# Part of an expert layer's start, moved into the last attention batch of a fused cross-attention and feed-forward kernel

## The chip, the cores and the metric

The kernel runs on one core of one Trainium2 chip. The metric is the device time of one execution in microseconds. The engines have one instruction queue each: TensorE (PE in the profile; PEld is its weight load), VectorE (DVE), ScalarE (ACT), GpSimd (POOL) and SyncE (SP, which issues most transfers). An engine takes its instructions in the order of its queue and waits on semaphores for the other engines.

## The reference, cut to what matters

The whole model is two layers on x (8 batches of 256 rows of 512 values). The change lies in the second layer: cross-attention with 16 heads, and then a feed-forward layer with two shared experts that run on every row and sixteen routed ones, of which each row takes its best two.

```python
def _attend(q, k, v):
    scores = einsum('bqnd,bknd->bnqk', q, k) * scale
    return einsum('bnqk,bknd->bqnd', softmax(scores), v)
x = x + (_attend(q, k_img, v_img)) @ Wo + bo      # q, k: RMS norm of projections

h = layernorm(x)
aff = sigmoid(h @ wa)                             # affinities, 16 experts
topk_p, topk_i = top_k(aff, 2)                    # shares are normalised
expert(h) = (gelu(h @ g + gb) * (h @ w1 + b1)) @ w2 + b2
x = x + h + sum(shared experts of h) + sum(shares * routed experts of h)
```

In the code `h @ g` and `h @ w1` are called the gate and up products, `gp` and `up`; the affinities' product is `lg` (logits).

## The kernel before, in words

The program has four stages one after the other: a long convolution, a quantised feed-forward layer, attention, experts. Only the last two are touched.

**Attention** (from 414 us to 820 us) is 64 steps, eight for each of eight batches; a step is four heads of one 128-row tile against 256 keys. Steps are counted here from 0, so the last batch is steps 56 to 63. All four compute engines are held to program order (`in_order`), so the order in which the Python loop calls the parts is the order of each queue. One turn n of the loop calls, in this order:

- `normalise` of step n-1: a reciprocal on DVE (`rden`), then POOL multiplies the 128x1024 probabilities `pr` by it;
- `scores` of step n: 4 products on PE into `sc`, then on DVE a maximum over them and its scaling (both are `mx`);
- `turn` of step n-2: 8 transposes of `pr` on PE into two PSUM tiles `pt`, copied to `pts` by DVE and ACT, one each;
- `exps` of step n: four exponentials on ACT from `sc` to `pr`, which need `mx`;
- in the first six turns of a batch, a sixth of the projections for the batch after it (`coming.middle`, `coming.end`): `k_mm`, `q_mm`, `v_mm` and transposes. The last batch has none to make;
- `Norm` and its factor: layer-norm statistics of the batch that was finished before (in turns 6 and 7 of a batch);
- `values` of step n-3, in every even turn: products `o` on PE, copied to `oT` by ACT;
- `project_out`, in every fourth turn: product `fo` on PE, added to `xs` by DVE, bias added by POOL.

[...]

Behind the loop come the last batch's `Norm` and the end of all attention pools.

**Experts.** 16 tiles of 128 rows make four blocks (`tb`) of 512. The work up to the routed experts is, in PE order: `tiles_in(0)` and `tiles_in(1)` (each row tile is normalised by DVE to `dxn`, transposed by PE to `dxT`, copied by ACT into `xT`), `logits(0)` (product `lgT`, DVE copy `lgs`, product `lg`), the first gate and up products `gate_up(0, 0, 0)`, `tiles_in(2)`, `logits(1)`, `tiles_in(3)`, `logits(2)`, `logits(3)`; then seven more gate and up products of blocks 0 and 1, and `down`. Between them the generator `route` is drawn piece by piece: affinities (`aff`), the two maxima (`hot`), ranks by PE (`rank`), slots, and 32 scatters by POOL. `gated` applies gelu on ACT and the product on DVE (`yT`). The eight units of shared work are named by block, expert and half, so (0, 0, 1) is the second half of expert 0 on block 0.

Pools: attention works in a pool `att` with two buffers of everything; the first batch uses `first` and `second`, left from the stage before. The experts' pools `moe`, `experts` and PSUM `psD` are opened when attention's are closed.

Of the kernel before, what the change touches and what calls it, by code (L numbers as in the profile page):

```python
# [8 lines left out]
F32 = mybir.dt.float32  # L9
# [62 lines left out]
def tile_kernel(ctx: ExitStack, tc: tile.TileContext, a: dict, out: bass.AP):  # L72
# [743 lines left out]
    def biased(pool, nm, i, tok, bias, pre, ss):  # L816

        nc.vector.tensor_tensor(pre[:, i, :], tok, bias, ALU.add)
        junk = pool.tile([P, D], F32, tag="junk", name=f"{nm}_junk{i}")
        nc.scalar.activation(  # L820
            junk, pre[:, i, :], AF.Square, bias=zero, accum_out=ss[:, i : i + 1]
        )
# [26 lines left out]
    class Batch:  # L849
# [23 lines left out]
        def middle(self, k):  # L873
            b = self.b
            T = [xs[:, i, b, :] for i in range(2)]
            if k == 1:
                r = self.root.newton()
                self.xn = []
                for i in range(2):
                    self.xn.append(self.qpool.tile([P, D], F32, tag="xn", name=f"cxn{b}{i}"))  # L880
                    nc.vector.tensor_scalar(
                        self.xn[i], T[i], self.mv[:, i, 0:1], r[:, i : i + 1],
                        ALU.subtract, ALU.mult,
                    )
# [194 lines left out]
    with tc.tile_pool(name="att", bufs=2) as ap_, tc.tile_pool(  # L1079
        name="psC", bufs=2, space=PSUM  # L1080
    ) as pc:

        attention = in_order(tc)
        attention.__enter__()
# [4 lines left out]
        class Step:  # L1089
            def __init__(self, batch, i, cp, p, oT):  # L1090
                self.batch, self.b, self.i, self.cp, self.p, self.oT = batch, batch.b, i, cp, p, oT
                self.nm = f"{batch.b}{i}{cp}{p}"

            def scores(self):

                kT, qT = self.batch.kT, self.batch.qT
                self.sc = pc.tile([P, 2, 2, S], F32, tag="sc", name=f"sc{self.nm}")
                for cc in range(2):
                    for rr in range(2):
                        rows = slice((2 * self.p + rr) * NHD, (2 * self.p + rr + 1) * NHD)  # L1100
                        c = 2 * self.cp + cc
                        nc.tensor.matmul(  # L1102
                            self.sc[:, rr, cc, :], lhsT=qT[rows, c, self.i * P : (self.i + 1) * P],
                            rhs=kT[rows, c, :], start=True, stop=True,
                        )
                self.mx = stat.tile([P, 4], F32, tag="mx", name=f"mx{self.nm}")
                nc.vector.tensor_reduce(  # L1107
                    self.mx, self.sc.rearrange("p r c k -> p (r c) k"), AX.X, ALU.max
                )
                times(self.mx, self.mx, -scale)  # L1110

            def exps(self):
                self.pr = ap_.tile([P, 2, 2, S], F32, tag="pr", bufs=4, name=f"pr{self.nm}")
                self.den = stat.tile([P, 4], F32, tag="den", name=f"den{self.nm}")
                for h in range(4):
                    nc.scalar.activation(  # L1116
                        self.pr[:, h // 2, h % 2, :], self.sc[:, h // 2, h % 2, :], AF.Exp,
                        bias=self.mx[:, h : h + 1], scale=scale, accum_out=self.den[:, h : h + 1],
                    )

            def normalise(self):
                rden = stat.tile([P, 4], F32, tag="rden", name=f"rden{self.nm}")
                nc.vector.reciprocal(rden, self.den)  # L1123
                flat = self.pr.rearrange("p r c k -> p (r c) k")
                nc.gpsimd.tensor_tensor(  # L1125
                    flat, flat, rden.unsqueeze(2).to_broadcast([P, 4, S]), ALU.mult
                )

            def turn(self):

                self.pts = []
                for rr in range(2):
                    pt = pc.tile([P, 2, 2, P], F32, tag="tr", name=f"pt{self.nm}{rr}")
                    for cc in range(2):
                        for k in range(2):
                            nc.tensor.transpose(  # L1136
                                pt[:, cc, k, :], self.pr[:, rr, cc, k * P : (k + 1) * P], ident
                            )
                    pts = ap_.tile([P, 2, 2, P], F32, tag="pts", bufs=8, name=f"pts{self.nm}{rr}")
                    if rr:  # L1140
                        nc.scalar.copy(pts, pt)  # L1141
                    else:
                        nc.vector.tensor_copy(pts, pt)
                    self.pts.append(pts)

            def values(self, before):

                pts = before.pts + self.pts
                cp, v = self.cp, self.batch.v
                op = pc.tile([P, 2, P], F32, tag="mm", name=f"o{self.nm}")  # L1150
                for cc in range(2):
                    for k in range(2):
                        for r in range(4):
                            d0 = (4 * (2 * cp + cc) + r) * NHD
                            nc.tensor.matmul(
                                op[r * NHD : (r + 1) * NHD, cc, :], lhsT=v[:, k, d0 : d0 + NHD],
                                rhs=pts[r][:, cc, k, :], start=(k == 0), stop=(k == 1),
                            )
                nc.scalar.copy(self.oT[:, 2 * cp : 2 * cp + 2, :], op)

        def project_out(b, i, oT):
            T = xs[:, i, b, :]
            fo = pc.tile([P, D], F32, tag="mm", name=f"fo{b}{i}")
            for c in range(DC):
                nc.tensor.matmul(  # L1165
                    fo, lhsT=oT[:, c, :], rhs=wsb["Wo"][:, c, :], start=(c == 0), stop=(c == DC - 1)
                )
            nc.vector.tensor_tensor(T, T, fo, ALU.add)
            nc.gpsimd.tensor_tensor(T, T, wsb["bo"], ALU.add)

        class Norm:


            def __init__(self, b):
                self.at = slice(2 * b, 2 * b + 2)
                for i in range(2):
                    st = stat.tile([P, 6], F32, tag="bn", name=f"d{b}_bn{i}")
                    nc.vector.bn_stats(st, xs[:, i, b, :])
                    nc.vector.bn_aggr(dmv[:, 2 * b + i, :], st)
                self.root = Root(dmv[:, self.at, 1], 1.0, ln_eps, f"d{b}")  # L1180

            def factor(self):
                nc.vector.tensor_copy(dr[:, self.at], self.root.newton())
# [4 lines left out]
        batches[1].kpool = batches[1].qpool = ap_  # L1188
        batches[1].psum = pc
        steps = []  # L1190
        for b in range(B):
            for i in range(2):
                oT = ap_.tile([P, DC, P], F32, tag="oT", name=f"oT_{b}{i}")
                steps += [(b, i, cp, p, oT) for cp in range(2) for p in range(2)]
        for n in range(len(steps) + 4):
            coming = None
            k = n % 8
            if n < len(steps):
                if k == 0 and 0 < steps[n][0] < B - 1:
                    batches.append(Batch(steps[n][0] + 1, (ap_, ap_), pc))  # L1200
                steps[n] = Step(batches[steps[n][0]], *steps[n][1:])
                if k < 6 and steps[n].b + 1 < B:
                    coming = batches[steps[n].b + 1]
            if 0 < n <= len(steps):
                steps[n - 1].normalise()
            if coming:
                coming.begin(k)
            if k == 7 and n > 8:
                finished.root.log()
            if n < len(steps):  # L1210
                steps[n].scores()
            if 2 <= n < len(steps) + 2:
                steps[n - 2].turn()
            if n < len(steps):
                steps[n].exps()
            if coming:
                coming.middle(k)
                coming.end(k)
            if k == 6 and n > 8:
                finished = Norm((n - 14) // 8)  # L1220
            elif k == 7 and n > 8:
                finished.factor()
            if 3 <= n < len(steps) + 3 and steps[n - 3].p:
                steps[n - 3].values(steps[n - 4])
            if n >= 4 and steps[n - 4].cp and steps[n - 4].p:
                project_out(steps[n - 4].b, steps[n - 4].i, steps[n - 4].oT)
        finished = Norm(B - 1)
        finished.root.log()
        finished.factor()
# [326 lines left out]
    for (tb, e, f), n in zip(rest, (2, 2, 3, 3, 3, 3, 2)):  # L1556
        gated(tb, e, f, gate_up(tb, e, f, shw[e]), yTs[tb])
        for _ in range(n):
            next(pieces)
# [148 lines left out]
```

## Time and profile before

Median of three runs: 1248.28 us (1248.28 to 1249.29). The execution that was profiled took 1249.04 us; its span in the trace, from the first to the last instruction, is 1247.3 us, so 1.7 us lie around the span.

Over the span PE is busy 95%, DVE 60%, ACT 43%, POOL 35%. In stretches around the change, busy microseconds of each engine and the granted PE clock as a share of full speed:

| stretch, us | what runs | PE | DVE | ACT | POOL | PE clock |
|---|---|---|---|---|---|---|
| 480 to 540 (60 us) | attention, middle batches | 59.60 | 40.76 | 33.34 | 19.51 | 1.00 |
| 758 to 810 (52 us) | attention, mostly the last batch | 46.06 | 39.06 | 28.79 | 23.85 | 0.90 |
| 810 to 822 (12 us) | end of attention | 8.59 | 4.34 | 0.96 | 2.61 | 0.81 |
| 822 to 835 (13 us) | first tiles, first logits, (0, 0, 0) | 12.19 | 5.70 | 4.61 | 0.28 | 0.92 |
| 835 to 850 (15 us) | other tiles and logits | 12.08 | 3.90 | 4.30 | 0.98 | 0.93 |
| 850 to 862 (12 us) | (0, 0, 1), begin of routing | 12.00 | 7.44 | 3.13 | 0.00 | 0.80 |
| 880 to 910 (30 us) | gate and up products, scatters | 30.00 | 18.37 | 2.06 | 22.98 | 1.00 |

A busy PE is not one at full speed: where the clock is under 1.00 the same products take longer.

### The profile page before, as it was taken

The numbers are of one execution on the slowest core, as the hardware profiler recorded it, in microseconds if no ns is written. First come the engines' busy times: TensorE is split into PE (matmuls) and PEld (weight loads), VectorE is DVE, ScalarE is ACT, GpSimd is POOL, SyncE is SP. The second block draws the span as 40 slices with busy tenths as digits, with TensorE's granted clock in tenths as the row PEclk, the third lists the DMA queues.
The fourth block names the chain that finished last, engine by engine and source line by source line (L and its number), as shares of the span: only waits on it lengthen the run. The fifth ranks groups of instructions, "written<-read, shape, count | busy, mean of one in ns | idle before, by whom it ended". The sixth has DMA issues, their size and how long they took to land. (4 is left out here: it accounts for less than half of the span.)

```text
span 1247.3 us, 16999 instructions
## 1 busy us (share of the span) xinstructions
PE 1180.6 (95%) x6053; PEld 734.7 (59%) x6053; DVE 744.1 (60%) x1574; ACT 531.7 (43%) x1218; POOL 435.3 (35%) x498
## 2 busy tenths in 40 slices
PE   5999998799989999999999999889999999999997
PEld 4677764455545455555555555554457777777443
DVE  5998995888864566867868667745531222222352
ACT  3447446778773455646455465522002111111000
POOL 5878883333311233333333324510671000000550
PEclk9999999899999999999999999888999999999999
DMA  7425320998000100000000000050577888885571
GB/s 266 144 63 179 115 60 4 347 291 229 1 1 14 38 1 1 18 18 1 18 1 19 1 1 1 1 185 1 205 257 254 279 285 293 294 298 188 168 245 36
DMA packets 121214, 150.38 MB, mean 121 GB/s; under 512 B 9561, under 2 KB 79705, under 8 KB 120610
## 3 DMA queue, kind: packets, MB, share of 16 engines
q1 hardware_dynamic: 106704, 112.84, 28.6%
q10 hardware_dynamic: 9298, 19.60, 4.4%
q0 software_dynamic: 5120, 16.78, 4.0%
q8 instruction: 50, 0.82, 0.3%
q14 instruction: 42, 0.34, 0.1%
HBM read 104.80 MB, written 44.40 MB: 120 GB/s over the span
## 5 line engine op out<-in xcount | busy, mean ns | idle before, releaser
L1125 POOL TENSOR_TENSOR pr<-pr,rden 128x1024 f32<-128x1024 f32 x64 | 121.3, 1895 | 183.8 <-DVE rden L1123 159.9
L674 PE MATMUL y<-kv,tp 128*128 128x288 f32 x640 | 161.7, 408 | 5.2 <-DVE wl L697 5.1
L674 PEld LDWEIGHTS y<-kv,tp 128*128 128x128 f32 x640 | 119.0, 190 | 42.6 <-PE y L674 10.1
L1116 ACT ACTIVATE pr<-sc,mx 128x256 f32<-128x256 f32 x256 | 117.9, 472 | 59.9 <-DVE mx L113 51.6
L1592 POOL DMA_INDIRECT yg<-yd,slot x32 | 33.6, 1049 | 237.0 <-DMA yd<-o_yo 220.3
L1511 PE MATMUL r_h<-r_xT,r_gu 128*128 128x256 f32 x512 | 113.3, 379 | 1.5 <-ACT r_xT L1501 1.5
L1511 PEld LDWEIGHTS r_h<-r_xT,r_gu 128*128 128x128 f32 x512 | 97.1, 190 | 21.0 <-issue 6.7
L1107 DVE TENSOR_REDUCE mx<-sc 128x4 f32<-128x1024 f32 x64 | 77.5, 1212 | 18.6 <-PE sc L1102 17.5
L1136 PE MATMUL pt<-ident,pr 128*128 128x128 f32 x512 | 72.5, 286 | 7.1 <-POOL pr L1125 5.1
L1102 PE MATMUL sc<-kT_T,qT_T 32*128 32x256 f32 x512 | 73.7, 405 | 2.4 <-ACT pr L1116 1.5
L1136 PEld LDWEIGHTS pt<-ident,pr 128*128 128x128 f32 x512 | 56.6, 144 | 30.1 <-issue 21.2
L1518 DVE SCALAR_TENSOR_TENSOR r_y<-r_h,eb,r_ge 128x256 f32<-128x256 f32 x32 | 15.5, 484 | 96.7 <-PE r_h L1511 96.7
L1141 ACT COPY pts<-pt 128x512 f32<-128x512 f32 x64 | 37.5, 586 | 82.6 <-PE pt L1136 82.5
L393 PE MATMUL f_hp<-w1q,f_xq 128*128 128x512 bf16 x256 | 64.1, 396 | 2.5 <-ACT f_h L402 2.5
L612 POOL TENSOR_TENSOR kv<-kx 128x2048 f32<-128x2048 f32 x16 | 57.6, 3601 | 12.7 <-ACT kx L598 12.7
L1102 PEld LDWEIGHTS sc<-kT_T,qT_T 32*128 32x128 f32 x512 | 44.4, 187 | 27.6 <-issue 20.0
L1517 ACT ACTIVATE r_ge<-r_h,gb 128x256 f32<-128x256 f32 x32 | 15.2, 474 | 104.0 <-PE r_h L1511 104.0
L457 PE MATMUL f_op<-w2q,f_hq 128*128 128x512 bf16 x256 | 59.4, 386 | 0.0
L843 PE MATMUL k_mm<-Wk_sb,cx 128*128 128x512 f32 x128 | 58.4, 599 | 0.0
L113 DVE SCALAR_TENSOR_TENSOR mx<-mx,ones 128x4 f32<-128x4 f32 x64 | 56.8, 887 | 2.2
L1165 PE MATMUL fo<-Wo_sb,oT 128*128 128x512 f32 x128 | 57.7, 593 | 0.0
L1527 PE MATMUL r_po<-r_w,r_y 128*128 128x512 f32 x128 | 57.6, 592 | 0.0
(475 smaller groups left out, 2269.8 us busy)
## 6 DMA issues: line engine op xcount, KB each, us to landing
xd<-blank SPq DMA_DIRECT2D x1, 15360.0 KB, 57.5
tp<-kpd SPq DMA_DIRECT2D x32, 256.0 KB, 3.3
r_gu<-in_rg SPq DMA_DIRECT2D x16, 512.0 KB, 5.5
r_gu<-in_rw SPq DMA_DIRECT2D x16, 512.0 KB, 7.2
r_w<-in_rw SPq DMA_DIRECT2D x16, 512.0 KB, 5.9
r_xr<-xd SPq DMA_DIRECT2D x16, 512.0 KB, 4.0
yd<-r_yo ACTq DMA_DIRECT2D x32, 256.0 KB, 5.6
yd<-blank SPq DMA_DIRECT2D x1, 5376.0 KB, 73.7
```

Of the source, the lines that this page charges most:

```text
L393: nc.tensor.matmul(dst, lhsT=self.xq[i][:, c, :], rhs=w1q[:, c, cols], start=(c == 0), stop=False)
L457: nc.tensor.matmul(op, lhsT=self.hq[i][:, c, :], rhs=w2q[:, c, :], start=(c == 0), stop=(c == FC - 1))
L612: nc.gpsimd.tensor_tensor(view(kv, 0, [[PAIRS, A * G], [HD, 4], [1, HD]]), view(kx, 0, [[EXT, A * G], [0, 4], [1, HD]]), view(kx, 0, [[EXT ...
L674: nc.tensor.matmul(y[:, ll, :, 0:PAIRS], lhsT=tp[:, dl : dl + P], rhs=view(kv, (m0 * G + hh) * PAIRS, [[G * PAIRS, B], [1, PAIRS]]), start ...
L843: nc.tensor.matmul(t, lhsT=lT[:, c, i * P : (i + 1) * P], rhs=w[:, c, :], start=(c == 0), stop=(c == DC - 1),)
L1102: nc.tensor.matmul(self.sc[:, rr, cc, :], lhsT=qT[rows, c, self.i * P : (self.i + 1) * P], rhs=kT[rows, c, :], start=True, stop=True,)
L1107: nc.vector.tensor_reduce(self.mx, self.sc.rearrange("p r c k -> p (r c) k"), AX.X, ALU.max)
L1116: nc.scalar.activation(self.pr[:, h // 2, h % 2, :], self.sc[:, h // 2, h % 2, :], AF.Exp, bias=self.mx[:, h : h + 1], scale=scale, accum_ ...
L1125: nc.gpsimd.tensor_tensor(flat, flat, rden.unsqueeze(2).to_broadcast([P, 4, S]), ALU.mult)
L1136: nc.tensor.transpose(pt[:, cc, k, :], self.pr[:, rr, cc, k * P : (k + 1) * P], ident)
L1165: nc.tensor.matmul(fo, lhsT=oT[:, c, :], rhs=wsb["Wo"][:, c, :], start=(c == 0), stop=(c == DC - 1))
L1511: nc.tensor.matmul(ps, lhsT=self.w[0][:, c, k, f * P : (f + 1) * P], rhs=self.xT[:, c, 0:n], start=(c == 0), stop=(c == DC - 1),)
```

## The change

It does four things.

1. **Work moved ahead.** A generator `ahead_of_experts` is stepped once in each turn from 56 to 65, right behind `exps` and ahead of `Norm`, `values` and `project_out`. In turns 56 to 61 it makes the tiles 0 to 11, two in a turn; `logits(0)` and `logits(1)` follow in turns 58 and 60, `logits(2)` in turn 62; nothing in 63; the two halves of `gate_up(0, 0, 0)` in turns 64 and 65. Behind the loop it makes `gate_up(0, 0, 1)`. What is left behind attention is the tiles 12 to 15, `logits(3)`, and the other products.
2. **Logits are copied** from PSUM (tag "mm") to the old buffer `u9` in SBUF by a DVE copy for each block, from which `aff` is made; before, they stayed in one PSUM tile.
3. **Pools.** The batches' tiles come from two sets with one buffer each, used in turn; `pr` has 3 buffers instead of 4, `pts` 6 instead of 8, `junk` is in bfloat16. The room goes to a pool `early`, which holds `xT0`, `xT1`, `xT2` and the first expert's gate weights (loaded at the start of attention).
4. **PSUM.** The first two gate and up products lie in attention's "sc" buffers; `psC` is closed, and `psD` opened in its place, only when `gated` has been called for both. The routing pieces are drawn one after each of these two and three after each later one.

```diff
-        junk = pool.tile([P, D], F32, tag="junk", name=f"{nm}_junk{i}")
+        junk = pool.tile([P, D], BF16, tag="junk", name=f"{nm}_junk{i}")
...
+    early = ctx.enter_context(earlies)
+    xTs = [early.tile([P, DC, TB], F32, tag="gu", bufs=3, name=f"xT{tb}") for tb in range(2)]
+    xTs.append(early.tile([P, DC, TB], F32, name="xT2"))
...
+    sets = [(fk, batch.qpool), (ok, oddq.__enter__())]
...
-                self.pr = ap_.tile([P, 2, 2, S], F32, tag="pr", bufs=4, name=f"pr{self.nm}")
+            self.pr = ap_.tile([P, 2, 2, S], F32, tag="pr", bufs=3, name=f"pr{self.nm}")
...
-                    pts = ap_.tile([P, 2, 2, P], F32, tag="pts", bufs=8, name=f"pts{self.nm}{rr}")
+                pts = ap_.tile([P, 2, 2, P], F32, tag="pts", bufs=6, name=f"pts{self.nm}{rr}")
...
+    def tile_in(t, pool, bufs):
+        ps = transposed(pc, normed(t, pool, bufs, f"dxn{t}"), f"dxT{t}", "tr")
+        j = t % (TB // P)
+        nc.scalar.copy(xTs[t // (TB // P)][:, :, j * P : (j + 1) * P], ps)
...
+    def logits(tb, pool, tag, bufs):
...
+        nc.vector.tensor_copy(lg[:, tb * n : (tb + 1) * n, :], ps)
...
+    def ahead_of_experts():
+        for tb in range(3):
+            for j in range(0, TB // P, 2):
+                for i in range(2):
+                    tile_in(tb * (TB // P) + j + i, sets[0][1], 2)
+                if tb and j == 0:
+                    logits(tb - 1, fk, "cx", 1)
+                yield
+        logits(2, fk, "cx", 1)
+        yield
+        yield
+        for f in range(2):
+            ps = pc.tile([P, 2, TB], F32, tag="sc", name=f"gu0_0{f}")
+            first_gu.append([ps[:, k, :] for k in range(2)])
+            yield from gate_up(0, 0, f, s0_gu, first_gu[-1])
...
             if coming:
                 coming.middle(k)
                 coming.end(k)
+        if len(steps) - 8 <= n < len(steps) + 2:
+            next(for_experts)
...
+    for _ in for_experts:
+        pass
...
     pieces = route()
-    tiles_in(0)
-    tiles_in(1)
-    logits(0)
-    gu = gate_up(0, 0, 0, shw[0])
-    tiles_in(2)
-    logits(1)
-    tiles_in(3)
-    logits(2)
-    logits(3)
+    for t in range(NTT - TB // P, NTT):
+        tile_in(t, mo, 6)
+    logits(3, mo, "ge", 2)
     next(pieces)
     yTs = [hidden_rows(tb) for tb in range(2)]
-    gated(0, 0, 0, gu, yTs[0])
-    next(pieces)
...
+    for f in range(2):
+        gated(0, 0, f, first_gu[f], yTs[0])
+        next(pieces)
+    psC.__exit__(None, None, None)
+    pd = ctx.enter_context(tc.tile_pool(name="psD", bufs=4, space=PSUM))
...
+    rest = [(tb, e, f) for tb in range(2) for e in range(SH) for f in range(EC)][2:]
+    for tb, e, f in rest:
+        gated(tb, e, f, gates(tb, e, f, shw[e]), yTs[tb])
+        for _ in range(3):
             next(pieces)
```

## The prediction, made before the changed kernel was run

> **What bounds the kernel now.** I read the page's rows by slices first: they say which engine sets the end.
>
> ```profile
> PE   5999998799989999999999999889999999999997
> PEclk9999999899999999999999999888999999999999
> ```
>
> Each digit is a slice of 31.2 us. PE is the wall nearly everywhere, and the chain that ended last is PE lines; only slices 24 to 28 (750 to 900 us) show dips. So time can be won there alone: idle PE, and products stretched at a low clock. The PE timeline around the last batch's first steps comes next: start, length, line, output and inputs, and in brackets the idle time before.
>
> ```profile
> 770.36 1.09 PE L1136 MATMUL pt<-ident,pr 128*128 128x128 f32 x8
> 771.38 1.08 PE L1155 MATMUL o<-pts,v 128*32 128x128 f32 x32
> 772.39 1.13 PE L1102 MATMUL sc<-kT_T,qT_T 32*128 32x256 f32 x8
> 773.86 1.27 PE L1136 MATMUL pt<-ident,pr 128*128 128x128 f32 x8 [0.33 <-POOL pr L1125]
> 775.90 1.66 PE L1102 MATMUL sc<-kT_T,qT_T 32*128 32x256 f32 x8 [0.77 <-ACT pr L1116]
> ```
>
> The scores of step 57 (772.39) are made before step 56's exponentials begin (773.91): PE runs a step ahead, as far as two `sc` buffers let it. What paces a step is in the rows of DVE, POOL and ACT:
>
> ```profile
> 773.74 0.68 DVE L1143 COPY pts<-pt 128x512 f32<-128x512 f32 x1
> 775.88 0.18 DVE L1123 RECIPROCAL rden<-den 128x4 f32<-128x4 f32 x1 [1.46 <-ACT pr L1116]
> 775.97 1.19 DVE L1107 TENSOR_REDUCE mx<-sc 128x4 f32<-128x1024 f32 x1
> 777.20 0.94 DVE L113 SCALAR_TENSOR_TENSOR mx<-mx,ones 128x4 f32<-128x4 f32 x1
> ...
> 776.23 1.89 POOL L1125 TENSOR_TENSOR pr<-pr,rden 128x1024 f32<-128x1024 f32 x1 [2.42 <-DVE rden L1123]
> ...
> 778.23 0.47 ACT L1116 ACTIVATE pr<-sc,mx 128x256 f32<-128x256 f32 x1 [1.64 <-DVE mx L113]
> ```
>
> `mx` takes 0.16 us where POOL is still; here it ends at 778.14, just as POOL's multiplication ends (778.12), and so in every step of this batch. The cycle is: exponentials 1.93, `rden`, POOL 1.89, `mx` let go, next exponentials: 773.91, 778.23, 782.62, 787.01, or 4.39 us, and 5.16 after the step with `fo`. PE needs less and waits. From 773.91 to step 63's exponentials at 805.53 are 31.6 us. Behind lie 3.0 us of PE idle before the last `pt`, 2.6 before the first `dxT`, and four waits of 0.8 for `lgs`.
>
> **The change, part by part.** Let E(n) be the start of step n's exponentials; E(56) = 773.91 stays, since the new work comes behind it.
>
> *PE is tied to DVE.* The two `dxT` of turn n stand on PE ahead of `o`, `fo` and the scores of step n+1, and wait for `dxn`, which stands on DVE behind `mx` and the `pts` copy of turn n. So PE can't run ahead any more, and the next scores become part of the path. From E(n): `pts` has the DVE to +0.5, the two `dxn` (0.54, 0.46 apart, behind one another at 827.93) end at +1.0 and +1.5; the two `dxT` (1.04 for both at 840.97; 0.15 from `dxn` to PE at 820.89) end at +2.1. Then scores 1.13, maximum 1.23, `mx` 0.16; the `pt` behind the scores and ACT's `pts` copy (1.0 and 0.5) end at the same time: E(n+1) = E(n) + 4.8. In an even turn `o` lies between: 5.8. POOL is done at +4.2, so `mx` is no longer what waits. ACT's two `xT` copies (0.59 each) lie behind the exponentials while it waits for `pt`: nothing.
>
> *Logits* in turns 58 and 60 add the way from `lgT` to the next product, 2.80 us (826.19 to 828.99 now, the 0.8 wait for DVE's `lgs` included): 8.6. The new DVE copy of 128x64 lies behind `lg`, beside `o`: nothing.
> *Turn 59 with `fo`:* PE ends `fo` at +5.7 behind `dxT`; DVE has its addition ahead of `rden`, POOL its bias (2.0 from the addition's start to the next `pr` now, 788.17 to 790.17) ahead of the multiplication of step 59, which ends at +9.6 and lets `mx` go: 9.75.
> *Turn 62:* logits without tiles, then `Norm` (1.9 us of DVE at 764.48 to 766.37) ahead of `rden`, POOL, `mx`: 6.5.
>
> Steps 56 to 62: 5.8 + 4.8 + 8.6 + 9.75 + 8.6 + 4.8 + 6.5 = 48.9 us, where 31.6 were: E(63) = 822.8, **17.2 us later**. It is the order on one queue that does it, not too much work: PE's own products in these steps are about 36 us.
>
> *Behind the steps* PE is dense at the durations of before: `fo` of turn 63 from 821.6 (3.5), `pt` 1.0, gate 3.4, `o` 1.0, `pt` 1.0, up 3.4, `o` 1.0, `fo` 3.5, (0, 0, 1) 6.9: to 846.4. The chain of the last tile (DVE 0.7, POOL 1.3, statistics, Ln, Exp, Newton, factor: 5.5 us from 819.6 to 825.05 now) hides under (0, 0, 1) with about a microsecond over. Tiles 12 to 15 take 2.9 with the last copy, `logits(3)` 2.85: `lg` ends at **852.2**, where it ended at 850.1. Both pieces of gates are then done that took 828.99 to 835.94 and 849.94 to 859.34.
>
> *The hand-over of PSUM.* In the built program the first product of (0, 1, 0) waits for DVE's `yT` of (0, 0, 1), as its buffer lies in the old "sc" room. In DVE's queue that `yT` stands behind the first routing pieces. From `lg`'s end: copy and exponential 0.8, DVE 0.29 and 1.75, `yT` 0.75 (ACT's table load of 1.28 and gelu hide under these), six rows of `hot` 2.7, `yT` 0.75: PE stands for **7.0 us**, until 859.2. Before, (0, 0, 1) covered this chain.
>
> *The clock behind that stall.* The rows now:
>
> ```profile
> 848.22 1.89 PE L1310 MATMUL lg<-sel,lgs 128*128 128x16 f32 x8 [0.81 <-DVE lgs L1308]
> 849.94 6.12 PE L1318 MATMUL gp<-xT,s_gu 128*128 128x512 f32 x8
> 855.90 3.60 PE L1324 MATMUL up<-xT,s_gu 128*128 128x512 f32 x8
> ...
> 778.20:782.60 4.40, 4.40 (x44) 0.50 0.00 0
> 796.60:801.00 4.40, 4.40 (x48) 0.61 0.00 0
> 850.00:856.00 6.00, 6.00 (x10) 0.59 0.00 0
> ```
>
> The last three are stretches: PE busy, then its granted clock. `gp` took 6.12 instead of 3.60 at a clock of 0.59. [...] The measurement decides: after the stall I take 2.5 (6.12 less 3.60). In the steps, half speed now falls into gaps of a chain that PE doesn't set; afterwards `dxT`, `o`, `lgT`, `lg`, `fo` and scores are the chain, some 26 of 48.9 us. At the 0.90 granted from 758 to 810 us that is 26 / 0.90 - 26 = 2.9 us; PE will be less full than it was there, so I go to 0.87, which gives **4**. Ends: 0 (the rule) and 9 (0.75, half of the time cold).
>
> So: 859.2 + 6.9 + 2.5 = 868.6 for (0, 1, 0), then `yT` and `both` 1.4, `rank` 1.1: ends at 871.1, where it ended at 867.3. That is +3.8, with the clock in the steps **+7.8**. From here both programs have the same: five gate pairs, `down`, scatters that start behind `yT` of (0, 1, 1), and PE full.
>
> *Edits at nothing.* Three `pr` and six `pts`: the step that frees each was transposed or multiplied on PE in an earlier turn, ahead of the scores that must come anyway; without that cover, one `pt` wait, about 1 us a step. Two sets instead of two buffers: each batch still writes beside the other one; context loads (3.6 us) have three steps of lead or more. SP: the first expert's gates load at the start of attention, with queues nearly empty (38 GB/s in that slice, 1 in the next); the second expert's are issued behind the last `fo` as now, and land (4 to 9 us) before 859. Loads for a routed expert move ahead of the first gather from `xd`; that was issued at 919.6 and has 5 us over before PE's 929.1, and landing takes 4.0: if it slips by more, PE waits for the rest. DVE gets no more in total but the four copies.
>
> **Sum:** 1249.04 + 7.8 = 1256.8 against the profiled execution's own time; the median lies 0.76 below that, so **1256** is what I name.
>
> **Rivals.**
> 1. *The gaps are filled, and it is faster than before.* If `dxn` is ready when PE reaches `dxT` (so scores aren't late), each step costs the larger of 4.39 and PE's own work: 4.4, 4.4, 5.9, 6.5, 5.9, 4.4, 4.9, 36.4 us and not 48.9, and a full PE stays at full clock: 12.5 + 4 less, **1240**. For it: PE's 11% of idle in 758 to 810 and 28% in 810 to 822, with DVE and ACT at 75% and 55%. Against: `dxn` cannot start before `mx`, which POOL holds. It decides where the new wait of PE in a step is under 0.3 us.
> 2. *The hand-over hurts little.* If the buffer is free when PE comes, `rank` starts when DVE's second `hot` is through, 10.8 after `lg`, and ends at 864: 7 less, **1249.5**. For it: now `yT` of the first product is through 3.3 us after `lg`. Against: the wait in the built program names the second.
> 3. *The half clock stays through the batch* (PE full for only two thirds of each step, below 773.9 to 782.6 now): 9 instead of 4, and a slow `fo` or gates, **1262**.
>
> **How the numbers follow.** The forecast 0.6, rival 1 0.1, rival 2 0.12, rival 3 0.18. This kernel can't be told from no change within 0.2%, 2.5 us. Rival 1 is faster; rival 2 straddles no change, 0.10 of it same and 0.01 on each side: faster 0.11, same 0.10, slower 0.79. The range goes from a little below rival 2 to above rival 3, since the clock term alone runs from 0 to 9: 1248 to 1264.
>
> **What would show it.** Right: exponentials of steps 57 to 63 some 4.8 to 9.8 us apart, PE idle on `dxn` in each turn 56 to 61, E(63) 17 us or more later; a PE idle of about 7 us before (0, 1, 0), on DVE; `rank` some 8 us later than 867.3 and the distance from there to the end as before. Wrong: steps still 4.4 apart, or PE idle on POOL as now; PE waiting on `r_xr` behind `down` would be a cost I have at nothing.

## The result, and the profile after

The changed kernel takes **1267.66 us** (median of four runs, 1265.66 to 1271.91) beside 1248.78 us for the kernel before on the same chip: ratio 1.0153, 95% interval 1.0133 to 1.0174. It is 18.9 us slower. Slower was forecast, but by 7.7 us: 1256, with a range to 1264. (Of all executions below, one ran slow, at 1382.03 us, of the first form under "Together", and is left out of its figures.)

The execution that was profiled is the slowest of the four, 1271.91 us with a span of 1270.2, so 22.9 us lie between the two spans. The slices first:

```profile
PE   5999998799989999999999997896989999999997
PEclk9999999899999999999999997688999999999999
```

The clock's slices 24 to 27, counted from 0 (762 to 889 us), read 7, 6, 8, 8; before, the dips were three slices of 8. Now the chain that ended last, in order of time, where the first new work stands (start, length, what):

```profile
769.11 1.88 DVE mx L113
770.99 0.60 DVE pts L1156
771.59 0.47 DVE dxn L1203
772.06 0.14 issue
772.20 1.46 PE dxT L160 x8
773.66 1.87 PE o L1168 x32
775.52 1.40 PE sc L1115 x8
...
776.95 1.24 DVE mx L1120
...
778.21 0.16 DVE mx L113
...
779.57 1.94 PE dxT L160 x8
```

This is the cycle that the prediction described, in its order: `pts`, `dxn`, 0.14 to PE, `dxT`, `o`, scores, maximum, the small `mx` of 0.16, and round again. The scores of the next step are on the path, and POOL is not, outside turn 59 with its bias, as forecast. What differs is the length of PE's pieces. The PE timeline of the same kernel (idle time before the instruction in brackets):

```profile
781.44 2.08 PE L1115 MATMUL sc<-kT_T,qT_T 32*128 32x256 f32 x8
...
786.19 1.94 PE L160 MATMUL dxT<-ident,dxn 128*128 128x128 f32 x8 [0.77 <-ACT pts L1154]
...
808.20 1.94 PE L160 MATMUL dxT<-ident,dxn 128*128 128x128 f32 x8 [3.06 <-DVE dxn L1203]
...
812.82 1.89 PE L1226 MATMUL lg<-sel,lgs 128*128 128x16 f32 x8 [0.81 <-DVE lgs L1222]
814.64 1.94 PE L1168 MATMUL o<-pts,v 128*32 128x128 f32 x32
```

Each of these products takes nearly twice its time at full clock (scores 1.13, `o` 1.08, `lg` 1.06, `dxT` 1.04), and the clock says why. In a stretch (length, then busy PE, its weight loads, DVE, ACT and POOL; the granted clock is third from the end):

```profile
808.00:838.00 30.00, 27.41 (x162) 18.84 (x163) 11.59 (x28) 9.75 (x34) 5.68 (x3) 0.51 0.00 1
```

A PE that is 91% busy looks like the limit here. It is busy because it runs at half speed: from 808 to 837 us the chain is PE's own products, but for two copies `lgs` by DVE and one `pts` by ACT.

One sign named in the prediction is only half there. PE waits on `dxn` in turns 56, 57 and 60 (3.55, 1.65 and 3.06 us). In turns 58, 59 and 61 it waits 0.77 us on ACT's `pts`, the copy behind `pt`: at half speed that way takes longer than the way over `dxn`, which the sum had at the same length.

Where the 22.9 us lie, from the two traces, with E(n) as in the prediction. (The first row is no gain of the change: in the eleven other changed kernels below, which do the same work up to there, E(56) lies anywhere from 769.8 to 774.1.)

| part | before | after | difference |
|---|---|---|---|
| up to E(56) | 773.9 | 771.1 | -2.8 |
| E(56) to E(63) | 31.6 | 66.9 | +35.3 |
| E(63) to the end of `rank` | 61.9 | 48.6 | -13.3 |
| from there to the end | 379.8 | 383.6 | +3.8 |

The hand-over, PE timeline of the changed kernel:

```profile
867.14 1.06 PE L1226 MATMUL lg<-sel,lgs 128*128 128x16 f32 x8 [0.81 <-DVE lgs L1222]
875.45 5.19 PE L1234 MATMUL gp<-xT,s_gu 128*128 128x512 f32 x8 [7.24 <-issue]
...
885.35 0.28 PE L1434 MATMUL rank<-both,ones 128*128 128x272 bf16 x1 [1.27 <-DVE both L1430]
```

PE stands 7.24 us before (0, 1, 0), and its first product then takes 5.19 instead of 3.60 us. The trace names no releaser ("issue"); the built program names DVE's `yT` of (0, 0, 1), and in the trace that `yT` ends at 875.36, 0.09 before `gp` starts.

### The profile page after: what moved, and what is told of

Same layout as the page of the kernel before. It is cut to its first block, busy times and chain, and to the rows that moved or that the text cites. A ratio compares the mean times of both kernels' runs of the same rounds, so it can differ in the third digit from the quotient of the medians.

```text
span 1270.2 us, 17001 instructions
## 1 busy us (share of the span) xinstructions
PE 1190.8 (94%) x6053; PEld 741.8 (58%) x6053; DVE 742.4 (58%) x1578; ACT 531.5 (42%) x1218; POOL 434.5 (34%) x498
## 4 chain that ended last, share of the span: by engine, by line
PE 69%; DVE 17%; ACT 7%; DMA 2%; issue 2%; POOL 2%; SPq 0%; ACTq 0%; DVEq 0%; POOLq 0%
PE r_h L1551 9%; PE y L674 5%; PE pt L1149 5%; PE v_mm L843 4%; PE q_mm L843 4%; PE r_po L1567 4%; PE sc L1115 4%; PE po L1383 4%; PE fo L1178 4%; PE gp L1234 4%; PE up L1234 4%; PE o_h L1551 2%; PE k_mm L843 2%; PE o L1168 2%; ACT f_junk L419 2%
## 5 line engine op out<-in xcount | busy, mean ns | idle before, releaser
L674 PEld LDWEIGHTS y<-kv,tp 128*128 128x128 f32 x640 | 119.0, 190 | 42.5 <-PE y L674 10.1
L1115 PE MATMUL sc<-kT_T,qT_T 32*128 32x256 f32 x512 | 77.1, 421 | 0.8 <-DVE xs L465 0.8
L1557 ACT ACTIVATE r_ge<-r_h,gb 128x256 f32<-128x256 f32 x32 | 15.1, 473 | 104.3 <-PE r_h L1551 104.3
L457 PE MATMUL f_op<-w2q,f_hq 128*128 128x512 bf16 x256 | 57.9, 379 | 0.0
L843 PE MATMUL v_mm<-Wv_sb,cx 128*128 128x512 f32 x128 | 57.6, 593 | 0.0
```

Source lines behind the costliest of these rows:

```text
L674: nc.tensor.matmul(y[:, ll, :, 0:PAIRS], lhsT=tp[:, dl : dl + P], rhs=view(kv, (m0 * G + hh) * PAIRS, [[G * PAIRS, B], [1, PAIRS]]), start ...
L843: nc.tensor.matmul(t, lhsT=lT[:, c, i * P : (i + 1) * P], rhs=w[:, c, :], start=(c == 0), stop=(c == DC - 1),)
L1115: nc.tensor.matmul(self.sc[:, rr, cc, :], lhsT=qT[rows, c, self.i * P : (self.i + 1) * P], rhs=kT[rows, c, :], start=True, stop=True,)
```

## The experiments

Three theories were to be told apart: **the order** (PE waits for a fresh `dxn` on every turn), **the clock** (these waits put PE to half speed, which then lengthens the path), **the hand-over** (one wait at the end). Against them: that the smaller pools slow attention, or that it is simply more work. The step lengths come first, from the starts of the exponentials on ACT; "clock" is the granted clock from E(56) to E(63).

| kernel | steps 56 to 62, us | sum | clock |
|---|---|---|---|
| before | 4.3, 4.4, 4.4, 5.2, 4.4, 4.4, 4.6 | 31.6 | 0.84 |
| *forecast at full clock* | 5.8, 4.8, 8.6, 9.75, 8.6, 4.8, 6.5 | 48.9 | |
| changed | 7.4, 7.5, 11.0, 10.1, 14.0, 6.6, 10.3 | 66.9 | 0.62 |
| drained behind the loop | 4.3, 4.4, 4.4, 4.6, 4.4, 4.4, 4.6 | 31.0 | 0.89 |
| 8 transposes a turn | 5.8, 4.8, 8.7, 9.6, 8.7, 4.8, 7.3 | 49.5 | 0.97 |
| 24 in turn 56 only | 5.8, 6.1, 11.0, 11.6, 11.7, 6.6, 7.0 | 59.7 | 0.74 |
| 16 a turn, `dxn` twice | 6.9, 6.0, 9.8, 10.8, 9.8, 5.9, 7.1 | 56.3 | 0.97 |
| 8 a turn, `dxn` twice | 8.1, 6.0, 9.8, 10.7, 10.8, 5.9, 6.6 | 57.9 | 0.94 |
| `dxn` a turn ahead | 5.3, 5.8, 5.2, 9.9, 4.5, 7.1, 4.3 | 42.2 | 0.88 |
| best, 12 transposes once | 4.4, 4.4, 6.0, 6.9, 6.2, 4.4, 5.2 | 37.6 | 1.00 |

### Nothing in the turns

```diff
-        if len(steps) - 8 <= n < len(steps) + 2:
-            next(for_experts)
```

> The generator is not stepped in the turns; all of its work comes behind the loop, with the pools, sets and PSUM of the changed kernel. Theory (the order of PE's queue ties the scores to dxn): steps 56 to 62 take 31 to 33 us as in the kernel before (66.9 in the changed kernel), PE waits on POOL again; behind them the tiles come back (+13 over the kernel before's hand-over and its stall of 7 us stays), so the whole is about 1257 us: 8 more than the kernel before, which is the hand-over with its stall. Rival (the cut pools, pr 3, pts 6, sets with one buffer, slow the steps): steps 56 to 62 stay above 40 us.

Measured: the steps take 31.0 us, so pools, sets and `pts` cost nothing in them, as forecast. The whole took 1261.34 us (ratio 1.0098, 1.0073 to 1.0124), 4 more than expected. From E(63) to `rank` are 76.8 us where 61.9 were: the stall is there (7.09 before a `gp` of 6.17 instead of 3.60, together 9.7), and the other 5 I hadn't counted: drained in one piece, the tiles have nothing beside them, and PE waits for `dxn` four times (0.8 to 1.3, 3.9 in all). In part the rest is half clock: two of the `lgT` took 1.70 us instead of 1.06.

### More work in the waits

```diff
     def tile_in(t, pool, bufs):
-        ps = transposed(pc, normed(t, pool, bufs, f"dxn{t}"), f"dxT{t}", "tr")
+        xn = normed(t, pool, bufs, f"dxn{t}")
+        ps = pc.tile([P, DC, P], F32, tag="tr", name=f"dxT{t}")
+        for c in range(8 if t < 12 and t % 2 == 0 else 0):
+            nc.tensor.transpose(ps[:, c % DC, :], ident, ident)
+        for c in range(DC):
+            nc.tensor.transpose(ps[:, c, :], xn[:, c * P : (c + 1) * P], ident)
```

> Eight transposes of the identity are added ahead of the two dxT in each turn 56 to 61, into the same PSUM tile, which dxT then overwrites: some 1.0 us of useless PE work a turn at full clock, at a place where PE waits. Theory (the gaps on DVE bring the half clock, and that costs 18 of the 66.9 us): PE waits less, the granted clock in 771 to 838 rises from about 0.6 to over 0.85, steps 56 to 62 take 50 to 57 us, and the whole 1252 to 1260 us, faster with more work. Rival (the steps are long because PE has too much to do): 6 x 1.0 to 1.9 us are added, 1274 to 1279 us, the clock unchanged.

Measured: 1254.34 us (1.0034, 1.0016 to 1.0052). Useless work made the kernel 13 us faster. Of the waits on `dxn` two are left, 1.70 us in turn 56 and 1.15 in turn 60. One turn of it on PE:

```profile
782.42 1.09 PE L1212 MATMUL dxT<-ident 128*128 128x128 f32 x8 [0.73 <-ACT pts L1154]
783.35 1.04 PE L1214 MATMUL dxT<-ident,dxn 128*128 128x128 f32 x8
...
786.19 1.06 PE L1231 MATMUL lg<-sel,lgs 128*128 128x16 f32 x8 [0.81 <-DVE lgs L1227]
```

At a clock of 0.97 the steps sum to 49.5 us, within 0.7 us of the forecast's 48.9 and each but the last within 0.15 of its own figure. So the order was sized right, and what is left goes with the clock: 66.9 less 48.9, or 18.0 us, in the profiled execution of the changed kernel. Two later kernels whose steps are those of the changed kernel (the first two of the hand-over) needed 61.6 and 63.3 at a clock of 0.70, so it is 13 to 18 us.

### Only the longest wait filled

The changed kernel waits on `dxn` for 3.55, 1.65 and 3.06 us. Only the first of these waits is filled here, to see whether the other two bring half clock as well.

```diff
-        for c in range(8 if t < 12 and t % 2 == 0 else 0):
+        for c in range(24 if t == 0 else 0):
```

> The changed kernel with 24 useless transposes (about 2.9 us) ahead of the first dxT of turn 56 alone, where PE stood for 3.55 us. Theory one (every wait on dxn can bring a stretch of half clock by itself, the 1.65 us one of turn 57 and the 3.06 us one of turn 60 too): the clock is full to about 778 and falls again behind turns 57 to 60; steps 56 to 62 take 57 to 66 us, the whole 1259 to 1266 us. [...]

```profile
769.81 2.84 PE L1212 MATMUL dxT<-ident 128*128 128x128 f32 x24 [0.68 <-ACT pts L1154]
...
778.45 1.07 PE L1214 MATMUL dxT<-ident,dxn 128*128 128x128 f32 x8 [1.65 <-DVE dxn L1203]
779.45 1.55 PE L1115 MATMUL sc<-kT_T,qT_T 32*128 32x256 f32 x8
780.93 1.97 PE L1149 MATMUL pt<-ident,pr 128*128 128x128 f32 x8
```

With the 3.55 us wait filled, PE is at full clock until the 1.65 us wait of turn 57, and half clock follows it: scores 1.55, `pt` 1.97. The whole took 1262.89 us (1.0118, 1.0098 to 1.0138), steps 59.7. Theory one holds: no wait in these steps is longer than 3.05 us, and the half clock comes, first behind 1.65 (0.50 from 782 to 786 us).

### A dearer dxn

```diff
         xn = normed(t, pool, bufs, f"dxn{t}")
+        if t < 12:
+            nc.vector.tensor_scalar(
+                xn, tile_of(t), dmv[:, t, 0:1], dr[:, t : t + 1], ALU.subtract, ALU.mult
+            )
...
-        for c in range(8 if t < 12 and t % 2 == 0 else 0):
+        for c in range(16 if t < 12 and t % 2 == 0 else 0):
```

> The changed kernel with sixteen useless transposes ahead of the dxT of each turn 56 to 61 (which keep the clock up), and each dxn of these turns made twice by DVE into the same tile. Theory (dxn is on the path of each step): about 1.0 us more for each turn than with the eight transposes alone (49.5 us for steps 56 to 62 there), 54 to 56 us, with the whole 4 to 6 us above that run: 1258 to 1261. Rival (PE's amount of work sets the steps, the wait is only where its slack shows): the 6 x 1.0 us of added transposes cost as much, but PE shows no wait on dxn; or neither costs, 1253 to 1256.

Measured: 1258.72 us (1.0074, 1.0057 to 1.009), steps 56.3, 6.8 more than with eight transposes. But in turns 57 to 59 and 61 PE showed no wait on `dxn`: sixteen transposes end just as late as the second `dxn`. In these turns the run decides nothing, so it was made again with eight.

> As the run with each dxn made twice, but with eight useless transposes a turn as in the first run with them, not sixteen: PE has the work of that first run, and only DVE has more (0.5 us for each second dxn, two a turn). Theory (dxn is on the path of each step): 0.9 to 1.2 us more a turn than with eight transposes and dxn once (49.5 us for steps 56 to 62 there), 55 to 57 us if the clock stays up, with a PE wait on dxn of about 1 us in each turn; more if the longer waits bring the half clock back (58 to 66 us). Rival (the sixteen transposes were what cost in that run): steps 56 to 62 stay within 1.5 us of 49.5.

Measured: 1259.01 us (1.0105, 1.0059 to 1.0151), steps 57.9. The PE waits of that run from 771 to 828 us (in total, times, longest):

```profile
PE dxT L1218 <- DVE dxn L1211: 6.9, 10, 2.3
PE dxT L1216 <- ACT pts L1154: 3.6, 5, 0.7
```

PE now waits on `dxn` in every turn. Turns 57, 58, 59 and 61 are longer by 1.17, 1.13, 1.14 and 1.14 us than in the run with eight transposes and `dxn` once; DVE's `dxn` of turn 57 take 2.16 us instead of 0.99, 1.17 more. Sixteen or eight transposes, these turns were the same within 0.02; it is DVE's microsecond that counts, one for one. Turns 56 and 60 lost 2.3 and 2.1, since half clock followed their longer waits (2.27 and 1.73): the `dxT` there took 2.15.

### The same work, one turn apart

```diff
+    def norms(n):
+        for t in (2 * n, 2 * n + 1):
+            if t < 12:
+                dxn[t] = normed(t, sets[n % 2][1], 2, f"dxn{t}")
+    def products(n):
+        if 0 < n < 7:
+            for t in (2 * n - 2, 2 * n - 1):
+                ps = transposed(pc, dxn[t], f"dxT{t}", "tr")
...
             steps[n].scores()
+        if len(steps) - 8 <= n < len(steps):
+            products(n - len(steps) + 8)
```

> dxn is made where it was, but its transposes and copies come one turn later, right behind the scores and ahead of pt, and each logits one turn later. Theory (it is the wait of PE for a fresh dxn, not the amount of work): PE no longer waits on DVE for dxn, steps 56 to 62 take 36 to 41 us at a granted clock over 0.85, E(63) comes 26 to 31 us earlier than in the changed kernel and the whole takes 1237 to 1243 us, less than the kernel before. Rival (the work itself fills DVE and ACT, or PE, so that the order doesn't matter): steps 60 us or more, 1262 us or more. Third (the half clock comes anyway, by the 0.8 us gaps at lgs): steps 45 to 55 us, 1246 to 1256.

```profile
798.85 1.13 PE L1115 MATMUL sc<-kT_T,qT_T 32*128 32x256 f32 x8
799.91 1.09 PE L160 MATMUL dxT<-ident,dxn 128*128 128x128 f32 x8
...
804.95 1.06 PE L1226 MATMUL lg<-sel,lgs 128*128 128x16 f32 x8 [1.56 <-DVE lgs L1222]
```

The waits on `dxn` are gone but for one (1.49 us in turn 57, with 10 us of half clock behind it), and the steps take 42.2 us instead of 66.9 with the same instructions. The whole took 1250.77 us (1.0018, 1.0004 to 1.0032): 17 less than the changed kernel, but not the 1237 to 1243 expected, and the steps are a little over the 36 to 41. It is no faster than the kernel before. The logits now wait longer (1.56 and 2.06 us) behind `mx` in DVE's queue, the stall of the hand-over is still there (7.15), and E(63) comes at 814.4 with more of PE's work still ahead of it, 52.2 us to `rank` instead of 48.6. I had taken the time of E(63) over to the end. (The total fits the third theory, but its cause does not: the half clock stands behind the 1.49 us wait, and none follows the waits at `lgs`.)

### The hand-over

```diff
     logits(3, mo, "ge", 2)
-    next(pieces)
     yTs = [hidden_rows(tb) for tb in range(2)]
     for f in range(2):
         gated(0, 0, f, first_gu[f], yTs[0])
+    for _ in range(3):
         next(pieces)
```

> Both gated calls of the first products come ahead of the first three routing pieces, nothing else changes. Theory (the first product of (0, 1, 0) waits for yT of (0, 0, 1), which stands in DVE's queue behind those pieces): PE's idle ahead of that product falls from 7.2 to about 2 us, the first gp behind it is at full clock (3.6 instead of 5.2 us), rank then follows 5 to 6 us earlier, and the whole takes 1261 to 1263 us. Rival (rank is held by DVE's own chain behind lg, or the time is lost again in front of down): rank moves by less than 2 us, 1266 to 1268 us.

Measured: 1259.96 us (1.0102, 1.0072 to 1.0132). From E(63) to `rank` are 42.2 us instead of 48.6. The wait fell to 1.68 as expected, but `gp`, which was to be at full clock, stayed at half:

```profile
865.24 5.14 PE L1234 MATMUL gp<-xT,s_gu 128*128 128x512 f32 x8 [1.68 <-POOL srow L1366]
```

(The POOL row is named because it came last by the profile; DVE's second `yT` ends 0.1 us before `gp` starts.) The next form gives the first product's `yT` earlier still:

```diff
+    gated(0, 0, 0, first_gu[0], yTs[0])
     for t in range(NTT - TB // P, NTT):
         tile_in(t, mo, 6)
-    logits(3, mo, "ge", 2)
+    gated(0, 0, 1, first_gu[1], yTs[0])
+    logits(3, mo, "xn", 6)
...
-        for _ in range(3):
+        for _ in range(1 if tb + f == 0 else 3):
             next(pieces)
```

> The changed kernel with gated of (0, 0, 0) ahead of the last four tiles and of (0, 0, 1) ahead of their logits, the copy lgs in another buffer, and one routing piece instead of three behind (0, 1, 0). Theory (the stall before (0, 1, 0) is DVE's order and nothing else, and the slow gp behind it is the half clock from that stall): no PE idle over 0.5 us ahead of (0, 1, 0), its gp takes 3.6 us, rank needn't be waited for, and from the exponentials of step 63 to rank's end are 46 us or less with 6.9 us more of gate products in front of rank (48.6 in the changed kernel), the whole 1257 to 1260 us. Rival (DVE's chain from lg to both sets rank and all behind it anyway): 1262 us or more.

Measured: 1259.54 us (1.0096, 1.0072 to 1.0121), 47.8 us from E(63) to `rank` with 6.9 us more of products in them, so 7.7 gained where 9.5 were expected. The wait before `gp` is 0.52, but the copy `lgs` now stands behind `yT`, `lg` waits 2.32 us for it, and `gp` is at half clock again: 5.05. I put that down to the wait of 2.32; the last run below speaks against it.

### Together

The form with `dxn` a turn ahead, `lgT` and `lg` a turn apart as well, and this hand-over:

```diff
+        if n in (3, 5, 7):
+            logits_out((n - 3) // 2)
...
+            if n in (2, 4, 6):
+                logits_in((n - 2) // 2, fk, "cx", 1)
```

> The parted form (dxn one turn ahead of its transposes) with lgT and lg parted by a turn too, in the turns where the changed kernel has its logits, and the order of the hand-over of the run before. Theory: E(56) to E(63) 36 to 40 us, no PE wait on lgs in the turns, no stall before (0, 1, 0); 9 to 11 us less than the parted form alone: the whole 1237 to 1241 us, less than the kernel before. Rival (the parted form has come down to what DVE and ACT can do, and what is won at the hand-over is lost in front of rank or down): 1246 us or more.

Measured: **1234.55 us** (0.989, 0.9868 to 0.9912). No wait on `lgs` in the turns, steps 40.8, a little over what was expected; the whole came out below it. The twelve transposes are then put ahead of the only `dxT` that still waits on `dxn`:

```diff
+                for c in range(12 if t == 0 else 0):
+                    nc.tensor.transpose(ps[:, c % DC, :], ident, ident)
```

> As the run before, with twelve useless transposes (about 1.5 us) ahead of the first dxT, in turn 57, where the parted form had its only wait on dxn (1.49 us) and behind it 10 us at half clock. Theory (the wait brings that stretch): no half clock from 772 to 784, 2 to 4 us less than the run before, 1234 to 1238 us. Rival (PE at half clock there is hidden behind the pace of DVE, POOL and ACT): no difference, or up to 1.5 us slower.

Measured: 1234.08 us (0.988, 0.986 to 0.9901). The half clock of turns 57 and 58 is gone and E(56) to `rank` is 3.3 us shorter (86.8 against 90.1), but the median moved only 0.5, less than the intervals can tell apart: in this profile E(56) itself comes 3.0 us later (772.8 against 769.8), in work that is the same. In this run the clock is full over the whole batch:

```profile
771.00:838.00 67.00, 62.43 (x492) 38.66 (x483) 41.22 (x79) 37.19 (x105) 21.27 (x30) 1.00 0.11 36
```

Its steps sum to 37.6 us; the prediction's first rival, in which the waits are filled, had 36.4. At the hand-over `gated` is now put between the copy `lgs` and the product `lg`:

```diff
-    gated(0, 0, 1, first_gu[1], yTs[0])
-    logits(3, mo, "xn", 6)
+    logits_in(3, mo, "xn", 6)
+    gated(0, 0, 1, first_gu[1], yTs[0])
+    logits_out(3)
```

> As the parted form with the handed-over PSUM and the twelve useless transposes, but gated of (0, 0, 1) between the copy lgs of the last logits and their product, so that this copy no longer stands behind yT. Theory: PE's wait of 2.3 us for lgs falls to 0.8, the half clock behind it (gp 5.5 instead of 3.6) goes, 2 to 3.5 us less: 1230.5 to 1232.5 us. Rival (the next wait, for yT, takes its place): 1233 to 1235 us, with PE waiting 1 us or more on yT ahead of gp.

Measured: **1232.71 us** (0.9857, 0.9841 to 0.9874), 17.8 us less than the kernel before beside it. `lg` waits 0.81 as expected, E(56) to `rank` is 84.3 instead of 86.8; but `gp` still takes 5.31, so the half clock that was to go stayed, now behind gaps of 0.68, 0.81 and 0.52 us. The next wait, on `yT` ahead of `gp`, is not the 1 us of the rival.

## Why the prediction was right in kind and wrong in size

- **PE tied to DVE, +17.2 us: right.** The chain shows the cycle in turns 56 and 57, the run with eight transposes its lengths (49.5 for 48.9), the dearer `dxn` its price one for one. Turn 62 was 0.75 short, 6.5 for 7.25.
- **Pools, buffers: nothing, right** for the last batch; the drained run shows it.
- **Behind the steps: right.** E(63) to the end of `rank` was 48.3 by the sum and is 48.6. In it the stall of 7.0 measured 7.24, and the slow `gp` behind it, put at 2.5, cost 1.6. But a slow `gp` needs no stall: the half clock begins at 868.29 us, when the stall is 0.1 us old, and with the wait cut to 1.68 or 0.52 us `gp` still took 5.05 to 5.31.
- **The clock in the steps, "which gives 4", is the step that failed.** It measured 18.0 in the profiled execution and 13 to 18 in three. The formula was nearly sound: 26 us of PE work on the chain at the measured 0.62 is 26 / 0.62 - 26 = 15.9; it leaves out `pt`, which at half speed joins the chain in turns 58, 59 and 61. The 0.87 put into it was not. I took it from 0.90 over 758 to 810 us, a stretch that began in full batches and in which PE ran a step ahead; and I gave 9 (a clock of 0.75) as the far end, when 0.50 to 0.61 stood in my own rows for short stretches at gaps of 0.33 to 0.81 us (and one of 1.21 us, at 795.29, ahead of the 0.61). What I missed is that the term feeds itself. Before, half speed was made up from PE's lead; now there is none, and from 808 to 837 us, behind the wait of 3.06, every product ran at half speed with gaps of only 0.77 to 0.81 us. Rival 3 named the mechanism, at half its price.
- **The lower end of the clock term, 0, rested on nothing that these runs show.** The term measured 18.0. With the 3.55 us wait of turn 56 filled no wait in the steps was over 3.05 us, and their clock was still 0.74: half clock first came behind a wait of 1.65 us there, and in the last form `gp` took 5.31 us instead of 3.60 behind gaps of only 0.68, 0.81 and 0.52.
- **Not in the sum at all:** 3.8 us behind `rank`. In `down` PE waits 1.82 and 1.37 us on DVE's `xs`, after DVE had stood 8.6 us ahead of the last `yT`, which the trace puts down to no engine of the core ("remote"). Five profiles have this stand of DVE (8.6 to 11.5 us: this one, the drained form, the eight transposes, `dxn` a turn ahead, the first hand-over), and of these two have the 3.2 us on PE, this one and the eight transposes; the other eight, the kernel before among them, have neither. No run was made on it; its cause stays open.
- **The sum, term by term,** for the profiled execution, which is 15.1 us over the 1256.8 of the sum: the clock in the steps 14.0 more, behind `rank` 3.8, the hand-over 0.3, and 2.8 less ahead of E(56), which is no part of the change; together 15.3, so these terms close the account.
- The rivals: filled gaps (1) did not happen in this change, but do when it is ordered otherwise; the cheap hand-over (2) did not (by its own sum it is 1249, not 1249.5). The rows by slices dip in slices 6, 7 and 11 too, in stages that the change leaves alone.

## What to carry to other kernels

Work put into an engine's idle time belongs behind what is already computed: if the moved product waits for an operand made in the same turn, the engine loses its lead, and the wait enters every turn. Price such a turn a second time with PE at half clock (here 1.94 us instead of 1.04 for `dxT`), for the products that are then on the path. Part the operand and its product by a turn (here 42.2 us for the steps instead of 66.9), and release a PSUM buffer before the long queue of another stage, not behind it (here a wait of 1.68 us instead of 7.24).

## What the runs showed of the hardware

- Eight transposes a turn that nobody reads, 1.0 us of work, took 13 us off the median, and the granted clock in the steps rose from 0.62 to 0.97. In the run with 24 of them PE made only transposes, useless ones and `dxT`, from 769.80 to 773.21 us, and the clock stayed at 1.00.
- Waits on `dxn` of 3.55, 3.06, 2.27, 1.73, 1.65 and 1.49 us were followed by half clock; in the run with eight transposes waits of 1.70 and 1.15 were not. In these runs the length alone doesn't decide.
- From 769 to 885 us of the changed kernel the granted clock was 0.50 in five stretches, from 772.72, 779.54, 793.20, 806.85 and 868.29 us, for 3.41, 10.24, 6.83, 30.72 and 10.24 us, and 1.00 between them. Rows around the first two, and around the begin of the last, at the end of the last `lg` (the second number is busy PE, the third from the end the clock):

```profile
769.31:772.72 3.41, 0.53 (x5) 0.56 (x6) 3.19 (x4) 1.63 (x7) 1.66 (x1) 1.00 0.00 0
772.72:776.13 3.41, 3.41 (x41) 2.52 (x41) 0.18 (x1) 1.73 (x5) 1.89 (x1) 0.50 0.02 5
776.13:779.54 3.41, 1.79 (x16) 1.20 (x12) 2.56 (x5) 1.58 (x6) 0.00 (x0) 1.00 0.00 0
779.54:782.95 3.41, 3.38 (x16) 2.75 (x16) 0.52 (x2) 2.03 (x6) 1.89 (x1) 0.50 0.00 0
...
864.87:868.29 3.42, 2.13 (x16) 1.12 (x16) 0.73 (x2) 0.34 (x1) 0.00 (x0) 1.00 1.04 295
868.29:871.70 3.41, 0.00 (x0) 0.00 (x0) 2.75 (x4) 3.06 (x4) 1.26 (x1) 0.50 1.08 376
```

- In the 3.41 us ahead of each of the five stretches PE was busy 0.53, 1.79, 2.60, 1.70 and 2.13 us. That share alone doesn't decide either: 1.72 us busy in the run with eight transposes (769.98 to 773.40) and 1.60 in the changed kernel (933.14 to 936.56) were followed by full clock.
- Gaps of 0.8 us did not end a stretch at half: from 808.20 to 837.57 us of the changed kernel no gap of PE was longer than 0.81 us, and the clock stayed at 0.50. Nor did full work at once: from 813.68 to 820.50 us PE was busy 6.81 of 6.82 us, and it stayed at half. What brings the full clock back isn't settled.
